# Attention over selected rows: compact keys with a PSUM bank per head, one softmax pass over three key tiles, values with the heads innermost

## The chip, the cores and the metric

The kernel runs on one core of a Trainium2 chip. The metric is the device time of one execution in microseconds; lower is better. The engines are named as in the profile: PE (TensorE), PEld (its weight loads), DVE (VectorE), ACT (ScalarE), POOL (GpSimd) and SP (SyncE, which here only issues DMAs).

## The reference, cut to what matters

The program is two layers of a gated decoder over x of 2 x 2048 x 512: cross attention, a feed-forward part that works on selected rows alone, cross attention again, and a quantized feed-forward part with a convolution. The change lies in the second of these, `_L0_ffn_ref`. It picks the 256 rows of each batch with the highest router scores, runs causal self-attention with 16 heads of 32 on them, and then a gated FFN.

```python
_, idx = jax.lax.top_k(scores, CAP)                # CAP = 256
x_sel = jnp.take_along_axis(x, idx[:, :, None], axis=1)
h = rmsnorm(x_sel, g1)
qkv = (h @ W_qkv.T).reshape(Bq, CAP, 3, H, HD)     # H = 16, HD = 32
q, k, v = jnp.moveaxis(qkv, 2, 0)
att = jnp.einsum('bqhd,bkhd->bhqk', q, k) / math.sqrt(HD)
mask = jnp.triu(jnp.ones((CAP, CAP), bool), 1)
att = jax.nn.softmax(jnp.where(mask, -jnp.inf, att), axis=-1)
o = jnp.einsum('bhqk,bkhd->bqhd', att, v).reshape(Bq, CAP, Dq)
x_attn = o @ W_out.T
h2 = rmsnorm(x_sel + x_attn, g2)
x_ff = jax.nn.silu(h2 @ W1.T) * (h2 @ W2.T) @ W3.T
out = x.at[jnp.arange(Bq)[:, None], idx].set(x_sel + x_attn + x_ff)
```

## The kernel before

Stage 1 is the first cross attention with the router; it ends near 549 us. DVE then ranks the scores (L492, L514, L520), PE turns ranks into row indices `idx` (L541, L555), and POOL gathers the selected rows `xs` by indirect DMA (L557). There are 2 x 256 rows, four tiles of 128. `rms_block` normalizes them and writes them transposed into `hT`. From `hT` and the weights `wqkv` PE makes `v2` (L674).

The attention loop runs over `c`, four chunks of 128 channels, which are four heads of 32 each. A chunk makes queries `qc` and keys `pk` for both batches at once (L692, 16 matmul calls of 512 columns). ACT copies the keys into `kbs` (L702), a buffer with a copy of the keys per head in which all channels of other heads are zero; POOL clears it first (L687). So one matmul with all 128 rows gives the scores of several heads side by side. Then `b` runs over the two batches; I call one pair of c and b a unit, and there are eight. In a unit the queries 0 to 127 see only keys 0 to 127 (the causal mask): one call of 512 columns for four heads (`ps_q0`, L709). The queries 128 to 255 see all keys: two calls of 512 columns, each for two heads (`ps_q1`, L733). Each of the three results goes through a mask addition on DVE (L717, L741) and `softmax_rows`, which is a row maximum on DVE (L116), an exponential per head on ACT that also gives the sum (L119), a reciprocal on DVE (L127) and a product on POOL (L128). PE transposes the probabilities (L727, L751), DVE or ACT copies them (AT0 L728, AT1 L754), and PE multiplies them with `v2` (L759, L763): for each head in turn the first query half and then two key tiles of the second. ACT copies the result into `OT` (L770). The output projection `wout` (L775) and a second `rms_block` end the stage.

The FFN behind it makes `pu`, `pw` (L875) and `acc` (L861) for eleven slices f of the hidden size. Its weights w1c, w2c and w3c come in slots of three; the first three slices are loaded before the attention. Beside it the weights of the last part are quantized: `wr` tiles are loaded (L810, L814), ACT sums their absolute values (L819), and PE adds the sums over the partitions (`wtot`, L824). The weights of the second cross attention are loaded here too: `L_ctxT`, `L_wk` and `L_wv` (L157 to L161), and `L_wq`, `L_wo` and `L_bo` (L170 to L172, 2 MB, 2 MB and 256 KB); DVE scales `L_bo` (L173).

[...] The order on each engine is not that of the source: a scheduler in the language sets it from what depends on what and from the memory that tiles share. All loads stand on one queue, SP's, so a load that waits holds up those behind it. Tiles of different stages may share addresses, and then the later one waits until the earlier one is done. [...] the attention stage uses two for `mm`, two for `sc`, two for `tp` and two for `o`.

Of the kernel before, what the change touches and what calls it, by code (L numbers as in the profile page):

```python
# [17 lines left out]
P = 128  # L18
# [25 lines left out]
def flamingo_kernel(ctx: ExitStack, tc: tile.TileContext, a: dict, out: bass.AP):  # L44
# [552 lines left out]
    with ExitStack() as st:  # L597
# [46 lines left out]
        with ExitStack() as sa:  # L644
# [4 lines left out]
            ps_sc = psum_pool(sa, "s2_sc", 2)  # L649
            ps_tp = psum_pool(sa, "s2_tp", 2)  # L650
            ps_o = psum_pool(sa, "s2_o", 2)
# [11 lines left out]
            mask = w.tile([P, 2 * P], F32, name="mask")  # L663
            nc.gpsimd.memset(mask[:, 0:P], 0.0)
            make_causal_mask(nc, mask[:, P:], NEG)
# [18 lines left out]
            for c in range(DC):  # L684

                kbs = act.tile([P, B, 4, CAP], F32, name="kb", tag="kb", bufs=2)
                nc.gpsimd.memset(kbs, 0.0)  # L687
                qc = act.tile([P, BLK], F32, name="qc", tag="qc", bufs=2)
                pq, pk = [ps_mm.tile([P, BLK], F32, name=n, tag="mm") for n in ("pq2", "pk2")]
# [10 lines left out]
                for h in range(4):  # L700
                    r = slice(32 * h, 32 * h + 32)
                    nc.scalar.copy(  # L702
                        kbs[r, :, h, :], pk[r, :].rearrange("p (b k) -> p b k", b=B)
                    )
                for b in range(B):
                    kb = kbs[:, b]

                    ps = ps_sc.tile([P, 4, P], F32, name="ps_q0", tag="sc")
                    nc.tensor.matmul(  # L709
                        ps,  # L710
                        qc[:, ds(b * CAP, P)],
                        kb[:, :, 0:P],
                        start=True,
                        stop=True,
                    )
                    A0 = act.tile([P, 4, P], F32, name="A0", tag="A0", bufs=2)
                    nc.vector.tensor_tensor(  # L717
                        A0,
                        ps,
                        mask[:, P:].unsqueeze(1).to_broadcast([P, 4, P]),  # L720
                        ALU.add,
                    )
                    softmax_rows(A0, 4, P, act, row, A0)
                    AT0 = act.tile([P, 4, P], F32, name="AT0", tag="AT0", bufs=2)
                    tp = ps_tp.tile([P, 4, P], F32, name="tp0", tag="tp")
                    for h in range(4):
                        nc.tensor.transpose(tp[:, h, :], A0[:, h, :], ident)  # L727
                    nc.vector.tensor_copy(AT0, tp)  # L728

                    AT1 = act.tile([P, 2, 4, P], F32, name="AT1", tag="AT1", bufs=2)  # L730
                    for j in range(2):
                        ps = ps_sc.tile([P, 2, CAP], F32, name="ps_q1", tag="sc")
                        nc.tensor.matmul(  # L733
                            ps,
                            qc[:, ds(b * CAP + P, P)],
                            kb[:, ts(j, 2), :],
# [3 lines left out]
                        A1 = act.tile([P, 2, CAP], F32, name="A1", tag="A1", bufs=2)  # L740
                        nc.vector.tensor_tensor(  # L741
                            A1,
                            ps,
                            mask.unsqueeze(1).to_broadcast([P, 2, CAP]),
                            ALU.add,
                        )
                        softmax_rows(A1, 2, CAP, act, row, A1)
                        tp = ps_tp.tile([P, 2, 2, P], F32, name="tp1", tag="tp")
                        for kt in range(2):
                            for h in range(2):  # L750
# [608 lines left out]
```

## Time and profile before

| what | us |
|---|---|
| median of 3 runs (lowest to highest) | 1871.38 (1870.84 to 1874.89) |
| the profiled execution's own time | 1878.88 |
| its span, from the first to the last instruction | 1877.2 |
| rows gathered and normalized | 574 to 589 |
| v2, queries and keys of the first chunk | 589 to 612 |
| the eight units of attention and the output projection | 612 to 697 |
| second normalization | 697 to 707 |
| FFN of the selected rows | from 704 on |

The page gives busy time by engine, the time of groups of equal instructions and the waits between engines. A group's line reads: source line, engine, operation, tiles written and read, shapes, count, then the busy time in us and the mean of one in ns. A float32 matmul call leaves two records on PE, a transpose one. Matmuls are pipelined: the time from one start to the next says what a call costs, and a record's length is more than that. In the table of stretches each engine has its busy time and its count of records, then the granted PE clock (1.00 is full speed), the share of DMA and what it moved.

### The profile page before, as it was taken

Reading aid. Unit: us, or ns where it says so; the run is one execution under the profiler, and the core shown is the slowest. Engines: PE = TensorE matmul, PEld = TensorE weight load, DVE = VectorE, ACT = ScalarE, POOL = GpSimd, SP = SyncE. Lnnn points to the kernel's source line nnn. Section 1 sums busy time; section 2 is a strip of 40 time slices with the busy share of each in tenths; the row PEclk is TensorE's granted clock in tenths of the full one; section 3 lists DMA queues with packets and bytes.
Section 4 is the critical chain, followed back from the end, with each engine's and each line's share of the span. In section 5 each row is a group of like instructions: output and inputs, shape, how many; then the busy total and the mean of one; then the engine's idle time right before and its main releaser. Section 6 shows DMA issues by size and latency. Waiting matters only on the chain.

```text
span 1877.2 us, 24320 instructions
## 1 busy us (share of the span) xinstructions
PE 1684.7 (90%) x7580; PEld 845.9 (45%) x7626; DVE 1306.7 (70%) x2753; ACT 1063.0 (57%) x3085; POOL 529.8 (28%) x668
## 2 busy tenths in 40 slices
PE   6989988988836989998999999999999999898969
PEld 3544544544413444454544454544444444443423
DVE  5777787887783541324536879888888888876966
ACT  1745544254511653503626877888787787754556
POOL 4534424252301320023313332332423232230200
PEclk9999889799977999998999999999999999998989
DMA  7011011011122009621001233324134133155465
GB/s 284 1 46 46 1 46 45 10 48 46 46 95 101 1 1 325 194 54 63 23 18 51 96 115 124 126 102 159 55 128 134 71 115 118 76 200 188 163 226 189
DMA packets 98455, 184.34 MB, mean 98 GB/s; under 512 B 11328, under 2 KB 30528, under 8 KB 94615
## 3 DMA queue, kind: packets, MB, share of 16 engines
q1 hardware_dynamic: 97430, 180.70, 27.7%
q0 software_dynamic: 896, 2.10, 0.6%
q8 instruction: 60, 0.98, 0.2%
q14 instruction: 69, 0.56, 0.1%
HBM read 108.31 MB, written 74.45 MB: 97 GB/s over the span
## 4 chain that ended last, share of the span: by engine, by line
PE 36%; DVE 12%; DMA 6%; ACT 5%; issue 2%; POOL 2%; SPq 1%; POOLq 0%; DVEq 0%; ACTq 0%
PE pp L315 9%; PE pq L248 8%; PE ph L1002 3%; PE po L297 3%; PE sc L271 2%; DVE h L1018 2%; PE pu L875 2%; PE tp L289 2%; PE po L1231 2%; PE acc L861 2%; PE pw L875 2%; DMA x<-h_d 1%; DVE u L1012 1%; ACT A L119 1%; DVE AT L290 1%
## 5 line engine op out<-in xcount | busy, mean ns | idle before, releaser
L119 ACT ACTIVATE A<-sc,nmx 128x128 f32<-128x128 f32 x1024 | 363.4, 377 | 175.6 <-DVE nmx L116 151.3
L128 POOL TENSOR_TENSOR A<-A,rden 128x512 f32<-128x512 f32 x280 | 298.0, 1066 | 560.1 <-DVE rden L127 454.1
L315 PE MATMUL pp<-L_wo,OT 128*128 128x512 f32 x768 | 367.1, 612 | 13.2 <-DVE u L1012 5.3
L248 PE MATMUL pq<-xnT,L_wq 128*128 128x512 f32 x768 | 363.7, 620 | 0.2 <-ACT xnT L237 0.2
L248 PEld LDWEIGHTS pq<-xnT,L_wq 128*128 128x128 f32 x768 | 147.4, 199 | 162.1 <-issue 153.9
L119 ACT ACTIVATION_READ_ACCUMULATOR A<-sc,nmx 128x1 f32 x1024 | 220.0, 215 | 0.0
L290 DVE COPY AT<-tp 128x512 f32<-128x512 f32 x256 | 173.3, 678 | 62.7 <-PE tp L289 62.0
L116 DVE TENSOR_REDUCE nmx<-sc 128x4 f32<-128x512 f32 x256 | 169.4, 679 | 67.8 <-PE sc L271 67.8
L315 PEld LDWEIGHTS pp<-L_wo,OT 128*128 128x128 f32 x768 | 139.1, 195 | 160.1 <-issue 134.8
L1018 DVE SCALAR_TENSOR_TENSOR h<-u,cw,h 128x512 f32<-128x512 f32 x256 | 190.7, 780 | 5.3 <-ACT h L1014 4.9
L289 PE MATMUL tp<-ident,A 128*128 128x128 f32 x1024 | 166.4, 286 | 29.5 <-POOL A L128 27.3
L271 PE MATMUL sc<-L_kT,qT 32*128 32x128 f32 (+1 forms) x2048 | 167.1, 294 | 7.7 <-ACT A L119 5.1
L271 PEld LDWEIGHTS sc<-L_kT,qT 32*128 32x128 f32 (+1 forms) x2048 | 133.3, 191 | 89.4 <-issue 63.1
L289 PEld LDWEIGHTS tp<-ident,A 128*128 128x128 f32 x1024 | 121.3, 144 | 103.7 <-issue 49.8
L1231 PE MATMUL po<-w2q,hq 128*128 128x512 bf16 x501 | 120.9, 393 | 19.6 <-ACT hq L1211 8.4
L1014 ACT ACTIVATE h<-u,cb,cw 128x512 f32<-128x512 f32 x128 | 99.1, 809 | 65.0 <-DVE u L1012 58.0
L1002 PE MATMUL ph<-xiT,w1q 128*128 128x512 bf16 x477 | 123.4, 382 | 3.0 <-DVE u L1012 0.6
L297 PE MATMUL po<-AT,L_v 128*32 128x512 f32 (+1 forms) x512 | 116.7, 631 | 8.2 <-DVE AT L290 7.7
L305 ACT COPY OT<-po 128x512 f32<-128x512 f32 x96 | 55.8, 588 | 104.1 <-PE po L297 103.4
L1012 DVE TENSOR_TENSOR u<-ph,inv_b 128x512 f32<-128x512 f32 x128 | 85.1, 684 | 30.8 <-PE ph L1002 26.3
L1011 POOL COPY u<-carry 128x2 f32<-128x2 f32 x128 | 49.5, 388 | 196.0 <-DVE h L1018 166.0
L311 POOL TENSOR_TENSOR x<-x,L_bo 128x512 f32<-128x512 f32 x64 | 87.0, 1377 | 38.0 <-DMA x<-x_d 15.8
(221 smaller groups left out, 2224.2 us busy)
## 6 DMA issues: line engine op xcount, KB each, us to landing
h_d<-h SPq DMA_DIRECT2D x28, 1024.0 KB, 4.1
x_d<-x SPq DMA_DIRECT2D x64, 256.0 KB, 2.8
hf<-h_d SPq DMA_DIRECT2D x64, 256.0 KB, 3.4
x<-x_d SPq DMA_DIRECT2D x61, 256.0 KB, 4.3
x<-h_d SPq DMA_DIRECT2D x48, 256.0 KB, 5.0
x<-in_x SPq DMA_DIRECT2D x32, 256.0 KB, 5.4
xn_d<-xn SPq DMA_DIRECT2D x32, 256.0 KB
xf<-x_d SPq DMA_DIRECT2D x32, 256.0 KB, 4.0
```

What stands on the lines that cost most here:

```text
L116: nc.vector.tensor_reduce(nmx, sc, AX.X, ALU.max, negate=True)
L119: nc.scalar.activation(out_tile[:, h, :], sc[:, h, :], AF.Exp, bias=nmx[:, h : h + 1], accum_out=den[:, h : h + 1],)
L128: nc.gpsimd.tensor_tensor(out_tile, out_tile, rden.unsqueeze(2).to_broadcast([P, n, width]), ALU.mult,)
L248: nc.tensor.matmul(pq, W.wq[:, d, ts(e, P)], xnT[:, d, :], start=(d == 0), stop=(d == DC - 1),)
L271: nc.tensor.matmul(sc[h][:, t, :], qT[e % cpg][r, ts(t, P)], W.kT[r, b, e, :], start=True, stop=True,)
L289: nc.tensor.transpose(tp[:, t, :], A[:, t, :], ident)
L290: nc.vector.tensor_copy(AT, tp.rearrange("p t n -> p (t n)"))
L297: nc.tensor.matmul(po[h * dh : (h + 1) * dh, :], W.v[:, b, ts(hd, dh)], AT[c * hpc + h], start=True, stop=True,)
L315: nc.tensor.matmul(pp, OT[e][:, ts(i, P)], W.wo[:, e, :], start=(e == 0), stop=(e == nE - 1),)
L1002: nc.tensor.matmul(ph, w1q[:, d, ts(c, P)], xiT[g][:, d, :], start=(d == 0), stop=(d == DC - 1),)
L1018: nc.vector.scalar_tensor_tensor(z, u[:, ds(k, BLK)], cw[:, c, k : k + 1], z, ALU.mult, ALU.add)
L1231: nc.tensor.matmul(po, rows(c), w2q[:, c, :], start=(c == 0), stop=(c == HC - 1))
```

## The change

The zero-padded `kbs` goes; the keys are copied once, into a compact `kc`. The scores of a head come from the 32 rows of its own channels in `qc` and `kc`, with one PSUM bank per head (`sc`, four banks; the pool `o` is gone and `po` takes its bank from `tp`). A head's bank holds three tiles of 128 keys: tile 0 is the first query half against keys 0 to 127, tiles 1 and 2 are the second query half against all 256 keys. The mask has three tiles too. Mask addition and maximum run per head over 384 elements; the maximum is taken per tile, and those of tiles 1 and 2 are joined. Two exponentials per head follow (128 and 256 columns), one reciprocal for all, and three products on POOL, one for each tile. Tiles 0 and 1 of the transposed probabilities are copied by DVE, tile 2 by ACT. The values run over the tiles outside and the heads inside. A unit's values are written in the source after the next unit's scores and probabilities.

The tiles of the stage also take less SBUF. In the built program this moves three loads on SP's queue: `L_wq` stands directly ahead of g1, in front of the first w1c, `L_wo` ahead of `wqkv`, and `L_bo` behind `wout`; the scaling of `L_bo` stands on DVE ahead of the first `qc`. In the FFN the loads are in another order with regard to each other: w1c and w2c of the fourth slice, three `wr`, the w3c, five `wr`. `wtot` stands on PE after the second group of `acc` and three calls of `pw`, where it stood after the third group of `acc`. From the end of the FFN on the order on every engine is that of before.

```diff
-            ps_sc = psum_pool(sa, "s2_sc", 2)
+            ps_sc = psum_pool(sa, "s2_sc", 4)
             ps_tp = psum_pool(sa, "s2_tp", 2)
-            ps_o = psum_pool(sa, "s2_o", 2)
...
-            mask = w.tile([P, 2 * P], F32, name="mask")
-            nc.gpsimd.memset(mask[:, 0:P], 0.0)
-            make_causal_mask(nc, mask[:, P:], NEG)
+            mask = w.tile([P, 3, P], F32, name="mask")
+            nc.gpsimd.memset(mask[:, 1, :], 0.0)
+            for k in (0, 2):
+                make_causal_mask(nc, mask[:, k, :], NEG)
...
-                kbs = act.tile([P, B, 4, CAP], F32, name="kb", tag="kb", bufs=2)
-                nc.gpsimd.memset(kbs, 0.0)
+            def queries_keys(c):
                 qc = act.tile([P, BLK], F32, name="qc", tag="qc", bufs=2)
+                kc = act.tile([P, BLK], F32, name="kc", tag="kc", bufs=2)
...
-                for h in range(4):
-                    r = slice(32 * h, 32 * h + 32)
-                    nc.scalar.copy(
-                        kbs[r, :, h, :], pk[r, :].rearrange("p (b k) -> p b k", b=B)
-                    )
+                nc.scalar.copy(kc, pk)
+                return qc, kc
...
+            def selected_probabilities(qc, kc, b):
+                sc = [ps_sc.tile([P, 3, P], F32, name="sc2", tag="sc") for _ in range(4)]
+                for k, nk in ((0, 1), (1, 2)):
+                    for h in range(4):
+                        r = slice(32 * h, 32 * h + 32)
                         nc.tensor.matmul(
+                            sc[h][:, k : k + nk, :],
+                            qc[r, ds(b * CAP + k * P, P)],
+                            kc[r, ds(b * CAP, nk * P)],
                             start=True,
                             stop=True,
                         )
+                A = act.tile([P, 4, 3, P], F32, name="A2", tag="A2", bufs=2)
+                m3 = row.tile([P, 4, 3], F32, name="m3", tag="m3")
+                for h in range(4):
+                    nc.vector.tensor_tensor(A[:, h], sc[h], mask, ALU.add)
+                    nc.vector.tensor_reduce(m3[:, h, :], A[:, h], AX.X, ALU.max, negate=True)
+                nc.vector.tensor_tensor(m3[:, :, 1], m3[:, :, 1], m3[:, :, 2], ALU.min)
+                den = row.tile([P, 4, 2], F32, name="den2", tag="den2")
+                for h in range(4):
+                    for k, nk in ((0, 1), (1, 2)):
+                        nc.scalar.activation(
+                            A[:, h, k : k + nk, :],
+                            A[:, h, k : k + nk, :],
+                            AF.Exp,
+                            bias=m3[:, h, k : k + 1],
+                            accum_out=den[:, h, k : k + 1],
                         )
+                rden = row.tile([P, 4, 2], F32, name="rden2", tag="rden2")
+                nc.vector.reciprocal(rden, den)
+                for k, to in ((0, A[:, :, 0, :]), (1, A[:, :, 1, :]), (1, A[:, :, 2, :])):
+                    nc.gpsimd.tensor_tensor(
+                        to, to, rden[:, :, k : k + 1].to_broadcast([P, 4, P]), ALU.mult
+                    )
+                return A
+
+            def selected_values(A, c, b):
+                AT = act.tile([P, 3, 4, P], F32, name="AT2", tag="AT2", bufs=2)
+                for k in range(3):
+                    tp = ps_tp.tile([P, 4, P], F32, name="tp2", tag="tp")
                     for h in range(4):
+                        nc.tensor.transpose(tp[:, h, :], A[:, h, k, :], ident)
+                    (nc.scalar.copy if k == 2 else nc.vector.tensor_copy)(AT[:, k], tp)
+                po = ps_tp.tile([P, CAP], F32, name="po2", tag="tp")
+                for k, cols, kt in ((0, ds(0, P), 0), (1, ds(P, P), 0), (2, ds(P, P), 1)):
+                    for h in range(4):
                         nc.tensor.matmul(
+                            po[32 * h : 32 * h + 32, cols],
+                            v2[:, 2 * b + kt, ts(c * 4 + h, 32)],
+                            AT[:, k, h, :],
+                            start=(k < 2),
+                            stop=(k != 1),
                         )
+                nc.scalar.copy(OT[:, c, ts(b, CAP)], po)
+
+            behind = None
+            for c in range(DC):
+                qc, kc = queries_keys(c)
+                for b in range(B):
+                    A = selected_probabilities(qc, kc, b)
+                    if behind:
+                        selected_values(*behind)
+                    behind = A, c, b
+            selected_values(*behind)
```

## The prediction

> **What bounds the kernel now.** The page comes first: PE is busy 90% of the span, DVE 70%, ACT 57%. The change touches one stage of about 95 us (the attention of the selected rows), so I next asked for busy time by stretch, cut where the lines change: v2 and the first queries and keys, the eight units of attention, the output projection, and a piece of the FFN behind it.
>
> ```profile
> core 0: us, PE busy (x) PEld busy (x) DVE busy (x) ACT busy (x) POOL busy (x), PEclk, DMA share, GB/s
> 574.00:589.00 15.00, 3.73 (x16) 2.97 (x17) 3.79 (x9) 2.78 (x8) 7.15 (x8) 0.50 0.87 315
> ...
> 612.00:667.00 55.00, 54.76 (x269) 27.09 (x268) 30.70 (x63) 35.49 (x123) 21.64 (x20) 1.00 0.00 1
> 667.00:696.00 29.00, 28.93 (x145) 14.65 (x144) 12.02 (x24) 17.21 (x53) 6.68 (x7) 1.00 0.00 1
> ...
> 725.00:746.00 21.00, 16.59 (x39) 7.03 (x37) 1.18 (x2) 9.76 (x17) 0.00 (x0) 1.00 0.99 358
> ```
>
> From 612 to 696 PE has hardly a gap at full clock, while DVE is busy 51%, ACT 63%, POOL 34%, DMA nothing. PE sets the pace there. Its records by shape say with what; the timeline shows how a matmul with 32 rows behaves elsewhere.
>
> ```profile
> L733 PE MATMUL ps_q<-kb,qc 128*128 128x512 f32 x32 | 16.4, 606 | 0.0
> L759 PE MATMUL po<-AT,v 128*32 128x128 f32 x64 | 11.0, 285 | 0.0
> L751 PE MATMUL tp<-ident,A 128*128 128x128 f32 x64 | 10.0, 278 | 0.0
> ```
> ```profile
> 305.59 1.17 PE L271 MATMUL sc<-L_kT,qT 32*128 32x128 f32 x32
> ...
> 616.46 1.02 PE L709 MATMUL ps_q<-kb,qc 128*128 128x512 f32 x2
> 617.32 1.02 PE L733 MATMUL ps_q<-kb,qc 128*128 128x512 f32 x2
> 618.38 0.66 PE L727 MATMUL tp<-ident,A 128*128 128x128 f32 x4
> 618.87 1.02 PE L733 MATMUL ps_q<-kb,qc 128*128 128x512 f32 x2
> ```
>
> One matmul call leaves two records. Starts are 0.86 us apart for a call of 512 columns (616.46 to 617.32). The third fact is in the first line: sixteen calls of 128 columns with 32 rows each, four heads into four banks, take from 305.59 to 306.69, 1.10 us or 0.27 for four; one after the other at 0.86 / 4 = 0.21 each they would take 3.4.
>
> Last, the waits of PE and SP's issues, for what stands behind the stage:
>
> ```profile
> PE wtot L824 <- ACT wq L819: 4.5, 1, 4.5
> ```
> ```profile
> 714.57 0.70 SPq L170 DMA_DIRECT2D L_wq<-in_L_WqT  x1
> 724.46 0.34 SPq L614 DMA_DIRECT2D w3c<-in_W3T  x1
> 724.85 0.42 SPq L171 DMA_DIRECT2D L_wo<-in_L_WoT  x1
> 725.33 0.57 SPq L172 DMA_DIRECT2D L_bo<-in_L_bo  x1
> 725.94 8.88 SPq L810 DMA_DIRECT2D wr<-in_w1T  x8
> ```
> ```profile
> 746.08 0.39 PE L824 MATMUL wtot<-wsum,ones 128*128 128x8 f32 x2 [4.49 <-ACT wq L819]
> 746.33 8.81 PE L875 MATMUL pu<-h2T,w1c 128*128 128x512 f32 x16
> ```
>
> At 741.6 PE stands 4.5 us at wtot, which needs the sums of all eight wr tiles. These are loaded behind L_wq and L_wo (2 MB each) while DMA is full (0.99). The sixteen records behind it take 8.6 us to the next group where they should take 16 x 0.43 = 6.9: the clock is 0.5 for one piece of 3.4 us. The wait costs 4.5 + 1.7 = 6.2.
>
> [...] PE gaps of 2.45 us and one of 1.70 (1216.6 to 1218.3) also stand beside pieces at 0.5.
>
> **The change part by part** (eight units: four chunks c, two batches b).
>
> *Scores.* Away go three calls of 512 columns, 3 x 0.86 = 2.57 us of PE a unit. In come four of 128 and four of 256, in parallel by four: 0.27 + 0.54 = 0.8. PE saves 1.77 x 8 = 14.2. The 256-column form isn't in the trace: at best 0.6 a unit, at worst in series the old 2.57.
> *Keys.* Sixteen kb copies of 0.58 on ACT become four kc copies of 0.59, and the POOL memsets (4 x 1.81) go. The first unit waits for one copy (0.6) and not four (2.34): 1.7 us earlier, as the first score stood at 612.76 behind keys done at 610.2. Two mask operations on POOL (0.22 and 0.30) are added near 577, beside the gather's landing (581): nothing; if not covered, 0.5.
> *Mask and maximum.* 3 + 3 DVE operations of 512 elements (0.69, 0.68; starts 0.60 apart) become 4 + 4 of 384: between 0.37 for 256 elements (L537) and 0.69, so 0.55, starts 0.46 apart. 8 x 0.46 = 3.7 against 3.6, and one small min (0.17) for two reciprocals less. Two AT copies go to DVE (1.2) where it had one, one to ACT where it had two.
> *Exponentials and scaling.* Eight a unit as before (128 columns 0.385 apart, 256 columns 0.49): 3.5. POOL's three products (1.04) remain, but all now wait for one reciprocal after all eight.
> *Values.* Twelve calls, before already some 0.95 a unit [...]; 3 x 0.27 = 0.8 now. Nothing taken; 1 us in all at most.
> *PSUM.* sc takes four banks, so the next unit's scores follow the adds one by one; po shares two banks with tp.
>
> Load of a chunk of two units: PE 6.9 (queries, keys) + 1.6 + 6 groups of transposes x 0.55 = 3.3 + 1.8 = 13.6; DVE 11.2; ACT 9.6; POOL 6.2. Before a chunk took 18.9, 21.1 and 16.6 (first scores at 612.8, 631.6, 652.8, 669.4). PE won't reach 13.6: its queue is in order, and in the built program the next queries and keys stand between transposes that wait for POOL. I walk a middle chunk from the first add, t = 0: adds and maxima to 3.8; an old AT copy and the min to 4.6; exponentials to 6.8; reciprocal 7.2; POOL 8.4, 9.4, 10.45. PE does old values to 5.1, three of four query calls to 7.7, waits, transposes at 8.45 and 9.45, the last query call to 10.8, the third transposes to 11.3, values 11.9, two key calls 13.6, values 13.9, two key calls 15.6, six transposes of the second unit 16.4, the next scores 17.2. So 17.3 a chunk, 3.7 of it PE waits. The first has no old unit: 14.4. The last, ended by eight calls of the output projection (6.9): 24.3 from its first add. First add at 611.9 (before 613.9). End: 611.9 + 14.4 + 2 x 17.3 + 24.3 = 685.2, against 696.65: **11.4 less**.
>
> *Moved loads.* The stage's tiles end at byte 162,528 of a partition before (the second A1) and at 154,848 after (AT2), and L_wq begins at 161,760. Freed of that overlap, the scheduler places L_wq ahead of g1, L_wo ahead of wqkv and L_bo behind wout on SP's queue. L_wq waits for the last xn store, about 550.7. It, nine FFN tiles (2.36 MB) and L_wo make 6.55 MB; at the 0.358 MB/us of 725 to 746 that is 18.3 us, to 569, or 571 with L_wo issued after its slot's earlier landing. wqkv waits until 573.9 for idx, so the cover is DVE's ranking, 3 us long. Cost nothing; without the cover each us late is a us, at most 11.7 (both loads). L_bo lands near 590, its scaling stands on DVE ahead of qc at 606.8: nothing; when late, qc waits. Behind the stage, wr no longer stands behind 4.4 MB: the last five are issued after w3c (724.46 in old time), land by 734, ACT ends at 735.3; wtot stands three pw calls after the second acc group, 737.1. No wait: **6.2 less**, at least 3. What is late next is ACT, by a margin of 1.8 us. From the end of the FFN on every queue is ordered as before: a shift.
>
> Sum 17.6. [...] I take one such stretch of 6.8 us as at 1217.7: +3.4. So **14.2 less** than the profiled execution's 1878.88 us (span 1877.2, the rest launch). That execution is 7.5 us, 0.4%, above the median; the difference carries over: 1871.4 - 14.2 = 1857.2.
>
> **Rivals.**
> 1. *PE hides its waits* (the walk adds latencies that overlap): chunks near 14.5, three times 2.8 = 8.4 more, no half clock 3.4: 1845.4. For it, PE has 55 us of gap-free work now; against, the in-order transposes.
> 2. *Row groups don't overlap with 256 columns[...]*: 1.77 x 8 = 14.2 of the 17.6 come back, and with the half-clock stretch nothing is left: 1871. Against it, L271; for it, a form the trace lacks. Then the change doesn't do what it says, and little but the moved loads is left.
> 3. *Moved loads delay wqkv* by 6 us: 1863. For it only 3 us of margin; against, the gather's own landing (581) and hT (588.5) come before wqkv's first use at 589.
> 4. *Slower: half clock in the stage.* PE's idle share goes from 0 to a fifth[...]. Each us at half clock delays PE by 0.5. From 35 us at 0.5 on it eats all 17.6; 60 of the stage's then 100 us give +30 - 17.6: 1884. Against it, stages with gaps of like size ran mostly at 1.0.
>
> **How the numbers follow.** Likeliest 0.66; rival 1 0.12; 2 0.08; 3 0.06; 4 0.08. Rival 2 falls mostly within 0.2% (3.7 us, about what a measurement of this kernel tells from no change). Faster 0.66 + 0.12 + 0.06 + 0.02 = 0.86; same 0.06; slower 0.08. The range leaves out rival 4, most of 2 and the tail of 1, some 0.2 in all: 1845 to 1869; the likeliest's own is 1851 to 1864.
>
> **What would show it.** sc records of four heads starting together and a unit's scores near 0.8 us; first scores of chunks 14 to 18 us apart; PE busy about 80% in the stage; a granted clock of 1.0 but for a piece or two; L_wq and L_wo issued before 562; no wait at wtot. Wrong if scores take over 2 us, if wqkv's first use moves past 590, if the stage ends less than 5 us earlier, or if the clock falls for over 20 us.

## The result, and the profile after

The changed kernel takes 1857.10 us (median of 6 runs, 1854.16 to 1858.86) against 1870.17 for six runs of the kernel before beside it: a ratio of 0.9927, 95% interval 0.991 to 0.9944, so 13.7 us less. Its profiled execution took 1854.16 us, with a span of 1852.5. The spans differ by 24.7 us, more than the medians, since up to the end of the ranking, ahead of the stage, PE was at half clock for 77.7 us in this execution and for 105.4 in that of before; I therefore compare the two stages that the change touches, and for the whole the ratios.

First the stage, by stretch. The columns are busy time and records per engine, the granted PE clock, the DMA share and GB/s.

```profile
core 0: us, PE busy (x) PEld busy (x) DVE busy (x) ACT busy (x) POOL busy (x), PEclk, DMA share, GB/s
574.00:589.00 15.00, 12.47 (x35) 7.03 (x36) 5.15 (x10) 1.33 (x4) 1.04 (x1) 0.75 0.44 159
602.50:682.00 79.50, 74.06 (x495) 37.92 (x494) 47.00 (x102) 42.64 (x156) 24.34 (x24) 0.91 0.00 1
```

From the first score to the last record of the output projection it is 79.5 us where it was 83.9. PE is still busy for 93% of it, but the clock reads 0.91 and not 1.00: 13.7 us of the stretch are at half clock. The groups of the stage with shapes kept apart say what became of the operations (mean ns of one at the end of the third part):

```profile
L737 POOL TENSOR_TENSOR A<-A,rden 128x512 f32<-128x512 f32 x24 | 24.3, 1042 | 72.1 <-DVE rden L735 72.1
L721 DVE TENSOR_TENSOR A<-sc,mask 128x384 f32<-128x384 f32 x32 | 16.5, 548 | 6.1 <-PE sc L711 5.2 <-PE tp L747 0.9
L722 DVE TENSOR_REDUCE m<-A 128x3 f32<-128x384 f32 x32 | 16.3, 543 | 0.1
...
L711 PE MATMUL sc<-kc,qc 32*128 32x256 f32 x64 | 9.0, 395 | 0.0
L711 PE MATMUL sc<-kc,qc 32*128 32x128 f32 x64 | 8.0, 321 | 1.8 <-DVE A L721 1.8
```

The additions and maxima of 384 elements take 0.548 and 0.543 us (I had put them at 0.55), a product on POOL 1.04. Then PE's timeline: the first score, and parts of the second chunk and those behind it. Each line is a start, the time to the end of the last record, and what it waited for in brackets:

```profile
602.52 0.94 PE L711 MATMUL sc<-kc,qc 32*128 32x128 f32 x16
...
616.86 0.94 PE L711 MATMUL sc<-kc,qc 32*128 32x128 f32 x16
617.73 1.09 PE L747 MATMUL tp<-ident,A 128*128 128x128 f32 x8
618.75 0.69 PE L711 MATMUL sc<-kc,qc 32*128 32x128 f32 x4
620.34 0.70 PE L711 MATMUL sc<-kc,qc 32*128 32x128 f32 x4 [0.90 <-DVE A L721]
620.97 0.43 PE L752 MATMUL po<-AT,v 128*32 128x128 f32 x8
621.33 0.92 PE L711 MATMUL sc<-kc,qc 32*128 32x128 f32 x8
622.33 0.98 PE L752 MATMUL po<-AT,v 128*32 128x128 f32 x16
623.23 4.15 PE L692 MATMUL pq<-hT,wqkv 128*128 128x512 f32 x6
...
629.49 0.64 PE L752 MATMUL po<-AT,v 128*32 128x128 f32 x16
630.06 1.99 PE L692 MATMUL pk<-hT,wqkv 128*128 128x512 f32 x4
631.97 0.43 PE L752 MATMUL po<-AT,v 128*32 128x128 f32 x8
...
640.46 1.08 PE L752 MATMUL po<-AT,v 128*32 128x128 f32 x16 [0.33 <-DVE AT L748]
641.47 5.27 PE L692 MATMUL pq<-hT,wqkv 128*128 128x512 f32 x6
...
661.17 3.96 PE L775 MATMUL pp<-wout,OT 128*128 128x512 f32 x6
```

Where nothing holds them up, the scores of a unit take 0.87 us (616.86 to 617.73: sixteen records, four calls of 128 and four of 256 columns). Where the four PSUM banks still hold scores that DVE has not added the mask to, they are broken up (618.75 to 622.2), since they then follow DVE's additions one by one, with 0.90 us of wait at 620.34. The three query calls at 623.23 and at 641.47 take 4.15 and 5.27 us, where three calls at full clock take 2.74 (625.26 in "padded keys" below): they lie in the pieces at half clock, and so does the projection's first group at 661.17 (3.96). Together these three groups lose 4.15 + 5.27 + 3.96 - 3 x 2.74 = 5.2 us. The values just ahead of each lose some 1.2 more: 0.90 us from start to next start at 622.33, 1.01 at 640.46 and at 660.16, against 0.57 at 629.49.

Last the loads on SP's queue, and `wtot` in the FFN:

```profile
541.54 0.38 SPq L170 DMA_DIRECT2D L_wq<-in_L_WqT  x1
...
552.20 0.43 SPq L171 DMA_DIRECT2D L_wo<-in_L_WoT  x1
565.60 1.47 SPq L654 DMA_DIRECT2D wqkv<-in_WqkvT  x3
567.11 0.76 SPq L658 DMA_DIRECT2D wout<-in_WoutT  x1
567.92 3.19 SPq L172 DMA_DIRECT2D L_bo<-in_L_bo  x1
```
```profile
722.16 0.28 PE L824 MATMUL wtot<-wsum,ones 128*128 128x8 f32 x2
```

Both 2 MB loads are issued before 553 and wtot has no bracket: PE did not wait for it. From the first transposes of the second normalization to the last `acc` it is 120.0 us, before 126.8.

### The profile page after: what moved, and what is told of

Same layout as the page of the kernel before. It is cut to its first block, busy times and chain, and to the rows that moved or that the text cites. A ratio compares the mean times of both kernels' runs of the same rounds, so it can differ in the third digit from the quotient of the medians.

```text
span 1852.5 us, 24500 instructions
## 1 busy us (share of the span) xinstructions
PE 1660.6 (90%) x7706; PEld 832.8 (45%) x7706; DVE 1311.2 (71%) x2769; ACT 1050.8 (57%) x3065; POOL 527.4 (28%) x666
## 4 chain that ended last, share of the span: by engine, by line
PE 34%; DVE 14%; DMA 6%; ACT 5%; issue 2%; POOL 2%; SPq 1%; POOLq 0%; DVEq 0%; ACTq 0%
PE pp L315 8%; PE pq L248 7%; DVE h L1018 3%; PE ph L1002 3%; PE sc L271 2%; PE po L297 2%; PE pu L875 2%; PE pw L875 2%; PE acc L861 2%; PE tp L289 2%; PE po L1231 1%; DMA hf<-h_d 1%; DMA x<-h_d 1%; DVE u L1012 1%; DMA hq<-hq_d 1%
## 5 line engine op out<-in xcount | busy, mean ns | idle before, releaser
L128 POOL TENSOR_TENSOR A<-A,rden 128x512 f32<-128x512 f32 x256 | 274.4, 1073 | 479.9 <-DVE rden L127 373.1
L315 PE MATMUL pp<-L_wo,OT 128*128 128x512 f32 x768 | 365.9, 610 | 12.7 <-DVE x L324 4.7
L248 PE MATMUL pq<-xnT,L_wq 128*128 128x512 f32 x768 | 358.0, 612 | 0.2 <-ACT xnT L237 0.2
L311 POOL TENSOR_TENSOR x<-x,L_bo 128x512 f32<-128x512 f32 x64 | 87.3, 1382 | 33.8 <-DMA x<-x_d 14.3
```

What stands on the lines that cost most here:

```text
L128: nc.gpsimd.tensor_tensor(out_tile, out_tile, rden.unsqueeze(2).to_broadcast([P, n, width]), ALU.mult,)
L248: nc.tensor.matmul(pq, W.wq[:, d, ts(e, P)], xnT[:, d, :], start=(d == 0), stop=(d == DC - 1),)
L315: nc.tensor.matmul(pp, OT[e][:, ts(i, P)], W.wo[:, e, :], start=(e == 0), stop=(e == nE - 1),)
```

## The experiments

All were run beside the kernel before, in several batches whose medians of it differ (1867.85 to 1872.36); the ratios are each to its own batch and can be compared, the medians less well. "Stage" is from the first score to the end of the output projection, with the time at half clock in it; "FFN" is the stretch just named. Stage and FFN come from one profiled execution of each. The time at half clock in the stage differs between kernels, so a difference of stages contains it.

| kernel | median us | ratio (95%) | stage | half clock | PE busy | FFN |
|---|---|---|---|---|---|---|
| before | 1870.2 | 1 | 83.9 | 0 | 83.6 | 126.8 |
| after | 1857.1 | 0.9927 (0.9910 to 0.9944) | 79.5 | 13.7 | 74.1 | 120.0 |
| loads back | 1866.8 | 0.9979 (0.9968 to 0.9990) | 79.1 | 13.7 | 74.1 | 129.1 |
| loads only | 1864.5 | 0.9962 (0.9948 to 0.9976) | 83.9 | 0 | 83.6 | 120.3 |
| values outside | 1864.4 | 0.9958 (0.9945 to 0.9971) | 84.6 | 10.2 | 79.8 | 119.1 |
| padded keys | 1858.8 | 0.9935 (0.9914 to 0.9956) | 82.0 | 0 | 79.3 | 119.0 |
| both | 1866.4 | 0.9971 (0.9960 to 0.9983) | 87.0 | 0 | 85.2 | 119.8 |
| keys ahead | 1854.9 | 0.9906 (0.9887 to 0.9925) | 76.1 | 3.4 | 69.2 | 120.0 |
| keys between | 1856.2 | 0.9908 (0.9882 to 0.9934) | 76.6 | 3.4 | 70.2 | 119.6 |
| split sums | 1856.7 | 0.9912 (0.9891 to 0.9933) | 76.5 | 3.4 | 69.3 | 120.5 |
| extra transposes | 1860.0 | 0.9929 (0.9905 to 0.9953) | 80.6 | 6.8 | 76.0 | 121.4 |
| padded, keys ahead | 1858.1 | 0.9931 (0.9908 to 0.9954) | 80.0 | 0 | 77.9 | 119.8 |
| split and ahead | 1852.4 | 0.9891 (0.9867 to 0.9915) | 78.6 | 13.7 | 74.4 | 118.7 |
| first unit padded | 1855.8 | 0.9933 (0.9915 to 0.9951) | 75.8 | 0 | 73.1 | 120.6 |

**Loads back.** The changed kernel with 8 KB of unused memory in the stage, so that the tiles reach over `L_wq`'s place again.

```diff
+            filler = act.tile([P, 2048], F32, name="filler")
+            nc.gpsimd.memset(filler[:, 0:1], 0.0)
             hT = wide("hT")
```

> The changed kernel with an unused tile of 8 KB in the stage's pool, so that the stage's tiles reach into L_wq's space again and L_wq, L_wo and L_bo are loaded in the FFN, as before the change. Theory A (the change is worth two separate parts: some 6.5 us in the FFN from the moved loads, some 6 us in the attention): PE waits about 4.5 us at wtot again with a half-clock piece behind it, and the kernel is 6 to 7 us slower than the changed one, near 1863.5; the attention stage stays as in the changed kernel (first scores to the last output projection near 79 us). Theory B (the FFN was shorter by luck of the clock, the attention is worth nearly all): within 2 us of 1857.

The wait is back, in PE's timeline of this kernel, and the loads stand behind the attention again, as SP's shows:

```profile
731.66 0.59 PE L827 MATMUL wtot<-wsum,ones 128*128 128x8 f32 x2 [5.35 <-ACT wq L822]
```
```profile
699.29 0.81 SPq L170 DMA_DIRECT2D L_wq<-in_L_WqT  x1
...
709.57 0.42 SPq L171 DMA_DIRECT2D L_wo<-in_L_WoT  x1
710.66 8.91 SPq L813 DMA_DIRECT2D wr<-in_w1T  x8
```

The FFN is 9.1 us longer than in the changed kernel and the whole 9.7 by the ratio: 5.35 us of wait, and 6.8 us at half clock behind it, which cost some 3.4. The stage is the same (79.1). The first theory holds, with a larger loss than the 6 to 7 us that it named.

**Loads only.** The kernel before, with the mask in a pool at the other end of the memory; nothing else.

```diff
+            w_right = sa.enter_context(tc.tile_pool(name="w_right", bufs=1, side="right"))
-            mask = w.tile([P, 2 * P], F32, name="mask")
+            mask = w_right.tile([P, 2 * P], F32, name="mask")
```

> The kernel before with its mask tile (1 KB) taken from the other side of SBUF, so that the attention's tiles end 256 bytes below L_wq; nothing else is changed. L_wq, L_wo and L_bo then stand on SP's queue behind wout, ahead of the attention. Theory A: no wait at wtot, 6 to 7 us faster than before, near 1863.5, the attention as before (84 us from first scores to the end of the output projection). Theory B: at most 2 us faster, above 1868.

The FFN is 6.4 us shorter than before, the stage is the same to 0.1 us, and the ratio of 0.9962 is 7.1 us: the first theory holds. So half of what the change brings has nothing to do with the arithmetic of attention: it comes of less memory in one stage. The loads did not get ahead of the attention in time, though, only in the queue's order:

```profile
684.93 0.37 SPq L170 DMA_DIRECT2D L_wq<-in_L_WqT  x1
685.35 0.51 SPq L171 DMA_DIRECT2D L_wo<-in_L_WoT  x1
```

`L_wq` still stands until the last product on POOL is done (at 684.98 in the trace of before, whose stage has the same times to 0.1 us). That is some 30 and 40 us ahead of their places before (714.57 and 724.85), in time in which the DMA queues had been idle (0.00 from 612 to 696), and `wr` no longer stands behind them; `wtot` has no wait (737.08).

**Values outside.** The changed kernel with the old order of the value products, heads outside.

```diff
-                for k, cols, kt in ((0, ds(0, P), 0), (1, ds(P, P), 0), (2, ds(P, P), 1)):
-                    for h in range(4):
+                for h in range(4):
+                    for k, cols, kt in ((0, ds(0, P), 0), (1, ds(P, P), 0), (2, ds(P, P), 1)):
```

> The changed kernel with the two loops of the values exchanged: heads outside, tiles inside, as before the change. Theory A (neighbours already ran in parallel, the exchange is worth 1 us in all at most): within 1.5 us of the changed kernel, 1856 to 1859. Rival (three calls of one column group in a row run one after the other, 0.2 us each, and values are on the path): a unit's values take 1.5 us or more in place of 0.6, eight times 0.9 = 7 us slower, near 1864.

PE's timeline of this kernel has the 24 records of a unit like this:

```profile
639.04 0.62 PE L752 MATMUL po<-AT,v 128*32 128x128 f32 x4
...
641.51 1.34 PE L752 MATMUL po<-AT,v 128*32 128x128 f32 x20
```

1.96 us where the changed kernel has 0.64 + 0.43 = 1.07 (629.49 and 631.97 above), and the stage grows by 5.2 us, the ratio by 0.0031 (5.8 us), with intervals that don't touch. The rival holds. The prediction had put this part of the change at nothing.

**Padded keys.** The changed kernel with the keys of before (four zero-padded copies on ACT, the clearing on POOL) and scores on 128 rows; mask and `v2` moved to the other end of the memory, so that the loads stay early.

```diff
-                            qc[r, ds(b * CAP + k * P, P)],
-                            kc[r, ds(b * CAP, nk * P)],
+                            qc[:, ds(b * CAP + k * P, P)],
+                            kc[:, b, h, 0 : nk * P],
```

> The changed kernel, but its scores come from zero-padded keys with 128 rows again (eight calls a unit, 128 and 256 columns, one after the other on the full array), with the four kb copies on ACT and the memset on POOL; mask and v2 lie on the other side of SBUF so that the moved loads stay moved. Theory A (PE sets the pace, row groups save 1.77 us a unit): a unit's scores take 2.6 us, chunks are 3 us or more longer, the first unit starts 1.7 us later, and of the stage's gain nothing is left: 10 to 16 us slower than the changed kernel, 1867 to 1873. Rival (the chain DVE, ACT, POOL sets the pace in the changed kernel and PE's saving went into waits): only the later start and ACT's copies show, 2 to 5 us slower, 1859 to 1862.

PE is busy for 5.2 us more than in the changed kernel (10 if the 5.2 us lost to half clock are set aside), but the stage is only 2.5 us longer, and the ratios, 0.9935 and 0.9927, can't be told apart. The first theory (10 to 16 us slower) is out. Where part of the rest went stands in PE's timeline of this kernel: the query calls run at full clock.

```profile
625.26 2.74 PE L694 MATMUL pq<-hT,wqkv 128*128 128x512 f32 x6
```

The six executions agree with the one that was profiled: the median of their mean clocks is 0.9535, in the changed kernel 0.9495 (0.951 to 0.954 in the batches of the kernel before).

**Both.** The two edits together.

> Both PE savings of the change are undone at once, the rest of it is kept: keys padded with zeros to 128 rows, and the value products with heads outside and key tiles inside. Singly, padded keys made the stage 2.5 us longer than the changed kernel's 79.5 and heads outside 5.2 us. Theory A: the first was small only because the in-order queue of PE and the half clock ate it, so both together cost more than the sum: PE busy in the stage near 90 us, the stage 87 to 91 us without half clock, median 1867 to 1871, slower than the kernel before with its loads moved (1864.5). Rival B: PE has room for both between its waits; the stage ends near 84 to 85, median 1863 to 1865, and the rest of the change (packed copies, widths, banks) is worth nothing either way.

The stage is 87.0 us, 7.5 longer than the changed kernel's, close to the sum of the single ones (2.5 + 5.2). That is the lower edge of the first expectation and clear of the second (84 to 85), but its reason isn't borne out: the two together cost the sum and not more, and PE is busy for 85.2 us and not near 90. Set against "loads only" (83.9), the rest of the rewrite (one pass over three tiles, a bank per head, DVE operations of 384 elements) costs 3.1 us of the stage. So within it: 3.1 lost, 2.5 and 5.2 won, 4.4 to 4.6 in all.

**Keys ahead, keys between.** If PE's order is what costs, the next chunk's queries and keys should go elsewhere: ahead of the second unit's scores, or (second version) between these and the old values.

```diff
+            ahead2 = queries_keys(0)
             for c in range(DC):
-                qc, kc = queries_keys(c)
+                qc, kc = ahead2
                 for b in range(B):
+                    if b == 1 and c + 1 < DC:
+                        ahead2 = queries_keys(c + 1)
                     A = selected_probabilities(qc, kc, b)
```

> The changed kernel with the queries and keys of the next chunk written ahead of the second unit of this one, so that they stand on PE before and not between that unit's transposes. Theory A (in the changed kernel the order on PE makes the gaps: key calls stand ahead of transposes whose inputs are ready, DVE waits 3.8 us for them twice, and the gaps bring half clock): chunks of 15 to 17 us where they are 18.1 and 19.4, fewer half-clock pieces in the stage, 4 to 10 us faster than the changed kernel, 1847 to 1853. Rival (the latency of the chain from scores to values sets the pace whatever fills PE): within 2 us of 1857.

> The changed kernel with the next chunk's queries and keys written behind the second unit's scores and probabilities and ahead of the first unit's values; the scores of a chunk's second unit then stand on PE ahead of those key calls. In the kernel that had the queries and keys one place earlier, DVE waited 5.2 us for the scores behind the key calls twice. Theory A (the order on PE makes the waits): that wait goes, the stage (first scores to the last output projection) takes 70 to 74 us where it took 79.5 in the changed kernel and 76.1 in that one; 1849 to 1853. Rival (the chain's latency sets the pace): the stage takes 75 to 78, 1853 to 1856.

**Split sums.** The two classes of width get tiles of their own for sums and reciprocals, and the four short exponentials come first, so POOL starts after four exponentials and not after eight.

```diff
-                den = row.tile([P, 4, 2], F32, name="den2", tag="den2")
-                for h in range(4):
-                    for k, nk in ((0, 1), (1, 2)):
+                den = [row.tile([P, 4, 1], F32, name="den2", tag=f"den2_{k}") for k in range(2)]
+                for k, nk in ((0, 1), (1, 2)):
+                    for h in range(4):
```

> The changed kernel with sums and reciprocals kept apart for tile 0 and tiles 1 and 2, so that POOL can scale tile 0 after the first four exponentials and not after all eight. Theory of latency (in the changed kernel POOL's late start sets when transposes come): POOL's first product starts some 2 us earlier in each unit, the stage is 3 to 8 us shorter, 1849 to 1854. Theory of order (PE has other calls placed ahead of the transposes in any case): within 2 us of 1857.

All three stages take 76.1 to 76.6 us, 3 us less than the changed kernel's, and each has 3.4 us of half clock where that has 13.7. For "keys between" the rival holds (75 to 78 us, against 70 to 74 if PE's order made the waits), for "split sums" the theory of latency at its lower edge in the stage (3 us) and the other in the total (1856.7), for "keys ahead" the total lies between the two. Three edits at three places that give one number suggest that what they share counts, and they share less half clock: 10.2 us less of it can be worth up to 5.1 us, more than the 3 that were won. So none of the three shows by itself that a wait was shortened. Over the whole run they are 0.0015 to 0.0021 lower in ratio than the changed kernel, inside the intervals, so this is shown in the stage and not in the total. DVE waits for scores for 15.2 us in the stage of the first version, 10.9 in that of the second and 5.2 in the changed kernel, and the stage doesn't follow these sums: that wait alone doesn't set its length.

**Extra transposes.** 24 useless transposes in the first three chunks, to keep PE busy.

```diff
-                    for h in range(4):
+                    for h in list(range(4)) * (3 if k == 2 and b == 1 and c < 3 else 1):
```

> The changed kernel with useless work on PE: the four transposes of tile 2 of each chunk's second unit (chunks 0 to 2) are done three times into the same bank. That is 24 more transposes of 0.11 us, 2.6 us of PE, at the place where PE waits 0.9 us for the adds of the next unit and after which the clock halves. Theory of the clock (the halving costs some 5 us of the stage and comes from PE's waits): half-clock time in the stage falls from 13.7 us to under 7, the stage is no longer than in the changed kernel or shorter, 1853 to 1857. Rival (the halving isn't tied to these waits): half clock stays near 13 us, the stage is 1 to 3 us longer, 1858 to 1860.

Half clock falls from 13.7 to 6.8 us, and the stage is 1.1 us longer. The work added costs about what the clock gives back, and a new wait at wtot (1.65 us) confuses the total: inconclusive as a remedy, and each of the two theories has one of its signs (half clock under 7 us; a stage 1 to 3 us longer). But it tells something on the cause, by the stretch of 3.4 us ahead of a piece at half clock and the piece itself:

```profile
619.00:622.40 3.40, 3.12 (x29) 1.86 (x31) 3.37 (x8) 2.30 (x9) 0.00 (x0) 1.00 0.00 0
622.40:625.80 3.40, 3.40 (x24) 1.82 (x25) 2.30 (x6) 2.73 (x11) 0.00 (x0) 0.50 0.01 2
```

PE is busy for 3.12 of 3.40 us, and half clock follows all the same. In the changed kernel, by the same view:

```profile
619.10:622.50 3.40, 2.42 (x32) 1.30 (x34) 3.40 (x9) 2.42 (x10) 0.00 (x0) 1.00 0.00 0
622.50:625.90 3.40, 3.40 (x19) 1.52 (x12) 3.37 (x9) 3.37 (x15) 0.96 (x1) 0.50 0.01 2
...
680.50:683.90 3.40, 1.48 (x4) 0.38 (x2) 0.69 (x1) 1.28 (x4) 0.00 (x0) 1.00 0.00 0
683.90:687.30 3.40, 1.25 (x7) 0.77 (x8) 1.84 (x5) 0.19 (x2) 1.01 (x1) 1.00 0.00 0
687.30:694.10 6.80, 6.17 (x15) 3.38 (x15) 2.91 (x4) 0.00 (x0) 0.00 (x0) 0.50 0.11 25
```

The stretch at 619.1 is idle for 1.0 us and followed by half clock; the one at 680.5, idle for 1.9 us, is not. The next, idle for 2.1 us and with nothing but transposes in it, is followed by half clock from 687.35 on. So idle time alone doesn't sort them. What the ones ahead of half clock within the stage have is scores: of the first stretch PE's `sc` records cover 1.96 us.

```profile
619.10:622.50 3.40, 1.96 (x16) 1.00 0.00 0
636.20:639.60 3.40, 1.75 (x16) 0.99 0.02 5
656.60:660.00 3.40, 1.82 (x16) 1.00 0.01 2
...
602.00:605.40 3.40, 2.25 (x24) 1.00 0.00 0
```

The first three are the stretches ahead of the three pieces. The last is the first unit's: it has more of the scores than any of them, and full clock follows. So the time of scores doesn't sort the stretches either. Whether half clock goes when such scores run on 128 rows is what "first unit padded" asks.

**Padded, keys ahead.** What the row groups are worth where PE's order is better.

> The version that issues the next chunk's queries and keys ahead of the second unit's scores (stage 76.1 us, median 1854.9), with keys padded to 128 rows. Theory A: where PE has other work for its waits, the shorter scores are worth most of the 11 us of PE that they save: the stage is 81 to 85 us long here and PE has hardly a gap, so the row groups are worth 5 to 9 us in that order of work against 2.5 in the order of the changed kernel; median 1860 to 1864. Rival B: they are worth the same 2.5 us in either order; stage 78 to 79, median near 1857.

The stage is 80.0 us, 3.9 longer than with compact keys, and PE has 2.1 us without work left. That lies between the two expectations, as the median does (1858.1): even here the shorter scores bring 4 us, not 11.

**Split and ahead.** Keys ahead and split sums together.

> Two edits on the changed kernel together: the next chunk's queries and keys ahead of the second unit's scores, and the sums of the two width classes in tiles of their own, so that POOL begins after the first four exponentials. Each alone brought the stage from 79.5 to about 76.3 us. Theory A: they fill the same waits, so together they bring little more than one: stage 75 to 76.5 us, median 1854 to 1856. Rival B: they fill different waits (one before the transposes, one before the scores) and add up: stage 72.5 to 74, median 1851 to 1853.

It has the lowest ratio of all, 0.9891 (0.9867 to 0.9915), some 20 us less than before; the interval still overlaps that of the changed kernel by a hair (0.9910 to 0.9944). The total is that of the second expectation, the stage that of neither: it is longer (78.6), with 13.7 us at half clock. The profiled execution was the slowest of the six (1861.55 us, at a mean clock of 0.944 where the others have 0.954 to 0.957), so its half clock need not be theirs. At full clock this stage would be up to 6.8 us shorter, near 72, and those of the single edits between 74 and 75, an estimate; whether the two edits fill different waits is not shown.

**First unit padded.** The kernel of "split and ahead", with padded keys for the first unit of each chunk alone.

```diff
-                        r = slice(32 * h, 32 * h + 32)
+                        r = slice(0, P) if b == 0 else slice(32 * h, 32 * h + 32)
...
-                            kc[r, ds(b * CAP, nk * P)],
+                            kc[0][:, h, 0 : nk * P] if b == 0 else kc[1][r, 0 : nk * P],
```

> The version with both edits (keys ahead, split sums; 13.7 us of half clock in the stage, stage 78.6 us, median 1852.4), with keys padded to 128 rows for the first unit of each chunk (b = 0) alone; the second unit keeps its row groups. In the runs so far each piece at half clock in the stage begins 3.4 us behind the start of a stretch that holds the 32-row scores of a chunk's first unit (1.5 us of them and more), with PE idle for 0.36 to 1.6 us of it, while stretches without scores that are idle for 1.4 to 1.95 us are followed by none, and the three kernels with padded keys show no half clock at all. Theory A: [...] with the first units padded the half clock falls from 13.7 to at most 3.4 us, the stage gets to 73 to 76.5 us although PE has some 5 us of scores more, median 1848 to 1852. Rival B: the idle time alone decides, which stays much the same around the other waits; half clock of 7 us or more stays, and the stage is 79 to 82 us, median 1853 to 1857.

No half clock is left in the stage, which is 2.7 us shorter than in "split and ahead" although PE has more to do. PE still waits as long as ahead of the halved pieces of "split and ahead" (0.50 and twice 0.90 us there):

```profile
618.49 2.41 PE L717 MATMUL sc<-kb,qc 128*128 128x128 f32 x12 [0.93 <-ACT A L733]
```
```profile
605.80:681.70 75.90, 73.10 (x495) 40.95 (x494) 46.34 (x110) 48.71 (x172) 26.46 (x26) 1.00 0.00 1
```

A wait of 0.92 or 0.93 us stands ahead of the scores in three of the chunks (618.5, 635.8, 653.1), and the clock stays at 1.00. For the clock and the stage the first expectation holds, in one profiled execution. The total does not follow: 1855.8 us and 0.9933 are above "split and ahead". A part of that is in the same profile: the FFN is 1.9 us longer (120.6 against 118.7) and has 8.5 us at half clock where the other has 5.3. From the end of the ranking to the last `acc` the kernel is then only 0.6 us shorter. For the executions without a profile only the mean clock of the whole is recorded: its median is 0.9515 here and 0.954 in "split and ahead" (whose profiled execution had 0.944), and within a kernel 0.001 less of it goes with some 1 us more (0.5 to 1.7 in the twelve experiments). So most of the 3.4 us between the medians goes with half clock somewhere in the program; why there is more of it here stays open.

**What stands ahead of half clock, counted over all fourteen traces.** In every trace the changes of the clock lie whole multiples of 3.41 us apart (in the changed kernel at 622.50, 625.91, 639.56, 646.39, 660.04, 663.46 and 687.35). From 598 to 698 us the fourteen traces have 383 stretches of this length at full clock, and 31 of them are followed by half clock. For each I added up PE's records at what they cost at full clock (0.43 us for 512 columns, in proportion for fewer) and weighted each by the share that its shape has of the largest one, 128*128: a score of 32*128 counts a quarter, a value product of 128*32 a quarter, everything else whole, transposes too. The weights are my choice; the sum, called use here, is an estimate from the records' shapes and starts.

| stretch | PE idle, us | use, us of 3.41 | clock behind it |
|---|---|---|---|
| after, 602.0 | 0.6 | 1.41 | full |
| after, 619.1 | 1.0 | 0.91 | half |
| after, 636.2 | 0.8 | 1.18 | half |
| after, 656.6 | 1.3 | 0.81 | half |
| after, 680.5 | 1.9 | 1.30 | full |
| after, 683.9 | 2.1 | 0.79 | half |
| extra transposes, 619.0 | 0.3 | 1.13 | half |
| first unit padded, 632.8 | 0.9 | 1.81 | full |

With a limit at 1.22 us this use puts all but one of the 383 on the right side; with its own best limit, idle time misses 16, rows alone 8, columns alone 17, and the use without transposes 15. The weights were not fitted, the limit was. Applied as it is to 60 to 540 us of the same traces (the first cross attention), it misses 19 of 1718, of which 140 are followed by half clock. So the use sorts these stretches; that the clock goes by it is not shown. This was counted after the fact; the one run whose half clock was forecast from the 32-row scores is "first unit padded", and it came out so (13.7 us to 0).

## Why the prediction was right, and where it was not

The total came out (1857.2 predicted, 1857.1 measured), but that it agrees to 0.1 us is luck: the interval of the ratio is 6 us wide, and the traces sum to 12.7 us where 14.2 were predicted. The moved loads, the earlier first unit and the times of the walk held. What the gain of the stage was put down to did not: the values, booked at nothing, bring 5.2 us; the scores, booked at 14.2 us of PE, bring 2.5; and the rest of the rewrite costs 3.1.

- **Moved loads: right.** 6.2 us predicted; 6.4 in the FFN of "loads only", 7.1 by its ratio, 6.8 from before to after. They cost nothing ahead of the attention: from the end of the ranking (L520) to the first transposes of `hn` it is 16.0 us before and 15.9 after.
- **The walk of the chunks: right at full clock.** Predicted first scores 14.4, 17.3 and 17.3 us apart and 25.15 from the last ones to the end (24.3 from the first add). Measured 14.3, 18.1, 19.4 and 27.6. Taking the 1.4, 2.5 and 1.2 us that the three halved groups lose off the last three gives 16.7, 16.8 and 26.4, and 74.3 us in all against 74.15; without the 1.2 us of the values ahead of them it would be 73.1.
- **Half clock: undersized.** One piece of 6.8 us and 3.4 us lost predicted, 13.7 us and 5.2 to 6.4 lost measured. That it comes with PE's gaps was my estimate from gaps of 2.45 and 1.70 us in the trace of before; over the fourteen traces idle time puts 16 of 383 stretches on the wrong side, the use as estimated above one. Rival 4 named the right danger at a size that did not come.
- **PE's load: misread, and with it the forecast of PE at 80%.** It is busy for 93%. My load for a chunk (13.6 us) counts calls by the distance of their starts and at full clock, while the busy time also has the ends of every broken-up group and the half clock in it. I put PE's waits at 3.7 us a chunk; the idle time of the whole stage is 5.4 us.
- **Values: the step that failed.** "Before already some 0.95 a unit ... 1 us in all at most." I had read the records from 621.12 to 622.2 as a unit. There are fourteen; the groups count 24 a unit (192 in eight), and the other ten stand at 624.50 to 625.3, behind keys and transposes:

```profile
621.12 0.41 PE L759 MATMUL po<-AT,v 128*32 128x128 f32 x2
...
622.14 1.13 PE L692 MATMUL pk<-hT,wqkv 128*128 128x512 f32 x2
...
624.50 0.30 PE L763 MATMUL po<-AT,v 128*32 128x128 f32 x1
...
625.28 0.66 PE L727 MATMUL tp<-ident,A 128*128 128x128 f32 x4
```

Before, a unit took 1.0 + 0.8 us, after it takes 0.57 + 0.36 from start to next start. Putting the old loop back costs 5.2 us of the stage. The total was not hurt, because the walk built the new stage from its own 0.8 and compared it with the measured end of the old one; the gain was only booked under another edit.

- **Scores: right as a price, wrong as a gain.** 0.8 us a unit predicted, 0.87 measured, so rival 2 is out. But the 14.2 us of PE "saved" are worth 2.5 us of the stage where the keys are put back alone: PE's busy time falls by 5.2 us against "padded keys" and not by 14.2, since broken-up scores and half clock (13.7 us against 0) stretch it, and part of that goes into waits for additions, POOL and copies. How much of the changed stage is held up by these waits and how much by half clock the runs do not tell apart.
- **First unit: right (1.5 us against 1.7).** From the first `pv` to the first score it is 23.6 us before and 22.1 after. Before, the first score is one call for four heads and starts at 612.76, just behind the fourth copy; after, it starts at 602.52, just behind the one copy. The lines are ACT's, the first of before, the second of after:

```profile
610.27 2.34 ACT L702 COPY kb<-pk 32x512 f32<-32x512 f32 x4 [6.34 <-PE pk L692]
```
```profile
601.77 0.58 ACT L700 COPY kc<-pk 128x512 f32<-128x512 f32 x1 [6.28 <-PE pk L692]
```

"Padded keys" has four copies again (601.54 to 603.92) and starts just as early (22.1 us), but its first score needs the copy of one head alone.

Sum of the traces: 1.5 (first unit) + 4.4 (stage) + 6.8 (FFN) = 12.7 us, against 14.2 predicted and 13.7 by the ratio.

DVE's additions show in the trace as a wait of PE's scores and not as the bound: PE waits for them three times in the stage, 1.8 us in all, 0.90 of it at 620.34.

## What to carry to other kernels

A gain in one engine's work is worth what the next chain leaves of it: put the old form back alone in the new structure before you book it, as two parts of this change had it the other way round: the one booked at 14 us of PE brought 2.5, the one booked at nothing 5.2. When a stage's tiles shrink, look at which loads the memory's overlap had held back; half of this gain was there, and one moved buffer in the old kernel brings it. Matmuls on few rows saved time here (0.87 us for a unit's scores, where before takes three calls of 0.86), and the eight kernels in which all scores run on 32 rows had 3.4 to 13.7 us of half clock in the stage; so where half clock shows, look at the shapes of the calls ahead of it and not only at gaps. Count the records of a group against the count of its line before you call a stretch of the timeline a unit.

## What the runs showed of the hardware

- Four calls of 32 rows into four banks overlapped with 256 columns as well as with 128: 0.87 us for four of each (changed kernel, 616.86 to 617.73). At 0.86 us for 512 columns they would take 2.6 one after the other, an estimate.
- Value products of 128 x 32: the 24 records of a unit took 1.07 us with the heads inside, where neighbours write different 32 rows of `po` (changed kernel), and 1.96 with the heads outside, where three in a row write the same ("values outside").
- Half clock came in pieces of 3.41 us (or several together), whole multiples of 3.41 us apart. Idle time of PE alone doesn't tell the stretches ahead of them: PE was busy for 3.12 of 3.40 us ahead of one piece ("extra transposes", 619.0), and another stretch with 1.9 us of idle time had none behind it (after, 680.5). An estimate of the use, time weighted by the share of rows and columns, with a limit near 1.2 of 3.41 us, sorts 382 of 383 stretches in the stage and 1699 of 1718 in the first cross attention. In the kernels whose scores use 128 rows, in whole or for each first unit (four), there was no half clock in the stage; in all eight changed kernels that keep the row groups there was 3.4 to 13.7 us. The padding also changes the order and the waits, and the limit was chosen on these traces, so this is a close fit and not a proof.
